# Silu in a convolution and attention block: one table function, or half the sum and its tanh

## Chip, cores, metric

One core of one Trainium2 chip. The metric is the device time of one execution in microseconds; several executions of the same program are run and their median is taken. A profile is of one execution.

Names used below: PE is TensorE, DVE is VectorE, ACT is ScalarE, POOL is GpSimd, SP is SyncE, whose queue issues nearly all DMAs. SBUF is the on-chip working memory, PSUM the eight banks that PE writes its products to. L130 is line 130 of the kernel.

## What is computed

Everything is fp32, on eight images of 512 channels and 32 x 32 positions. Layer 0 is a block of convolutions with attention, added to its input; layer 1 is a masked and permuted 1x1 convolution, also added to its input. Both take a group norm of their input first. Cut to what matters here:

```python
def cbs(x, w, p, pad):                       # convolution, batch norm in eval form, silu
    return silu(bn_eval(conv2d(x, w, pad), p))

def bot_attention(x, qkv_w, rw, rh):         # 4 heads of 64, 1024 positions
    q, k, v = conv2d(x, qkv_w, 0) ...
    logits = einsum('bhdi,bhdj->bhij', q, k + r) * HD ** (-0.5)
    return einsum('bhij,bhdj->bhdi', softmax(logits), v)

t = cbs(x, cv1_w, cv1_bn, 0)                 # 512 -> 512 channels
ys = [t[:, :256], t[:, 256:]]
for i in range(2):
    yi = ys[-1]
    z = cbs(yi, m_cv1_w[i], m_cv1_bn[i], 1)  # 3x3
    z = bot_attention(z, m_qkv_w[i], m_rw[i], m_rh[i])
    z = silu(bn_eval(conv2d(z, m_cv2_w[i], 0), m_cv2_bn[i]))
    ys.append(yi + z)
return cbs(concatenate(ys), cv2_w, cv2_bn, 0)
```

Silu is s * sigmoid(s) with s = scale * x + bias, where scale and bias come from the batch norm of the channel. It stands behind four convolutions: cv1, the 3x3 convolution of each of the two blocks, the 1x1 convolution behind each attention, and cv2.

## The kernel before

The 128 partitions carry channels; the free dimension carries positions, in halves of 512, as a PSUM bank holds 512 fp32 numbers. An image's activations that live longer go through buffers in device memory (`y_dram`, `x2_dram`).

*The slots.* Each image passes two attention blocks; a slot is one block of one image, and images run in pairs, so that there are 16 slots. A slot has four units (`Unit`): one pair of heads and one half of the positions each. A unit runs eight steps `t`. `logits` (L428) makes two PSUM banks of logits on PE (L435), ACT copies them to SBUF (`st`, L441), and DVE keeps a running maximum (`mx`, L446). `top` and `spread` transpose the maximum, reduce it (L455) and spread it into PSUM as `mb` (L462). `soften` (L464) adds `mb` on DVE (L466), takes exp on ACT (L467) and sums on POOL (L470, L472). `values` multiplies with v on PE (L478). `finish` makes the denominators (L490), their reciprocal (L492) and the product into `q` (L493).

*The work between.* A slot's softmax runs for one image while the other work is fed in between its steps, from a list with estimated costs in microseconds (`slot_filler`, `advance`): for the next slot `conv3` (the 3x3 convolution by transformed rows, six products with additions on DVE, L262 to L297) and `project` (q, k and v); for the slot before `conv_m2` (L340); and, from a background list, `conv1` (L201) of later images, `conv2` (L366) and `last` of finished ones. So every kind of Silu falls between copies and exps of a softmax. The order in which each engine executes is fixed when the program is built. The first two images' `start_conv` (L841) runs ahead of any softmax.

*Silu.* `bn_silu` (L129) is one ACT operation, with scale and bias read from the columns of `bn_s` and `bn_b`. Its callers:

- `start_conv` and `conv1`: from a PSUM bank into a tile `t` (named y), which SP stores to `y_dram`; 8 per image, 512 elements each.
- `conv3`: in place on `z` in SBUF, 2 per block, 1024 elements each.
- `conv_m2`: from a bank into `t` (m2s), to which DVE then adds the residual (L354), into `ybuf` or `res`; 4 per block, 512 elements.
- `conv2`: from a bank into `t` (cv2s), to which DVE adds the residual (L380), before the statistics of the second group norm (L139); 8 per image, 512 elements.

That makes 28 per image, 224 in all. ACT evaluates functions from a table set that has to be loaded; where an operation needs another set than the one before, the built program has a load (ACT_TABLE_LOAD in the trace), shown under the line of the operation that it precedes: L130 or L467.

*Buffers.* `half_tile` (L71) gives tiles of 512 elements from the pool `tp`, which has three in turn; besides the callers above `finish` takes one for the reciprocal. The pool `wt` has three tiles of 544 elements for temporaries of `conv3`. Banks come from `ps_f`, five in turn.

*Parameters.* `small_parameters` (L496) makes `bn_s` and `bn_b` once, at the start.

Of the kernel before, what the change touches and what calls it, by code (L numbers as in the profile page):

```python
# [16 lines left out]
AF = mybir.ActivationFunctionType  # L17
ALU = mybir.AluOpType
# [7 lines left out]
IT = 2  # L26
F = 32
HW = F * F
HALF = 512
# [6 lines left out]
BN_CV1, BN_CV2, BN_M1, BN_M2, BN_ALL = 0, 4, 8, 12, 16  # L36
# [3 lines left out]
def conv_preact_kernel(ctx: ExitStack, tc: tile.TileContext, x, cv1, cv2, mcv1, qkv, mcv2, bn, rw, rh, conv, s_in, t_in, out):  # L40
    nc = tc.nc
    stt = nc.vector.scalar_tensor_tensor

    def pool(name, bufs, **kw):
        return ctx.enter_context(tc.tile_pool(name=name, bufs=bufs, **kw))
# [10 lines left out]
    wm = pool("wm", 1)  # L56
    gy = pool("gy", 4)
    gr = pool("gr", 2)
    tp = pool("tp", 3)
    wt = pool("wt", 3)  # L60
    ps_m = pool("ps_m", 1, space=PSUM)
    ps_o = pool("ps_o", 1, space=PSUM)
    ps_f = pool("ps_f", 5, space=PSUM)
# [1 line left out]
    def pair(p, tag, name):  # L65
        return p.tile([P, 2, HALF], F32, tag=tag, name=name)

    def bank(name):
        return ps_f.tile([P, HALF], F32, tag="bank", name=name)

    def half_tile(name):  # L71
        return tp.tile([P, HALF], F32, tag="t", name=name)
# [7 lines left out]
    def weights(name, shape, src):  # L80
        t = wp.tile([P, *shape], F32, tag="w", name=name)
        load(t, src)
        return t
# [42 lines left out]
    bn_s = const.tile([P, BN_ALL], F32, name="bn_s")  # L126
    bn_b = const.tile([P, BN_ALL], F32, name="bn_b")

    def bn_silu(dst, src, col):  # L129
        nc.scalar.activation(dst, src, AF.Silu, bias=bn_b[:, col : col + 1], scale=bn_s[:, col : col + 1])  # L130


    class GroupNorm:
# [42 lines left out]
    class Image:  # L176
# [24 lines left out]
        def conv1(self, h, tiles, order=(1, 0)):  # L201
            n = self.n
            for cp in order:
                w = weights(f"w_cv1_{n}_{h}_{cp}", (CT, 256), cv1[cp])
                for co in range(IT):
                    ps = bank(f"cv1_{n}_{cp}_{co}_{h}")
                    yield from accumulate(ps, [(w[:, k, ts(co, P)], tiles[k // 2][:, k % 2]) for k in range(CT)])
                    t = half_tile(f"y0_{n}_{cp}_{co}_{h}")
                    bn_silu(t, ps, BN_CV1 + IT * cp + co)
                    load(y_dram[n][cp][:, co, ts(h, HALF)], t)  # L210
# [7 lines left out]
        def conv3(self, i):  # L218
            n = self.n
            name = f"{n}_{i}"  # L220
            groups = ybuf.rearrange("p c r x -> p (c r x)").rearrange("p (g r x) -> p g r x", r=4, x=F)
            d = [groups[:, 0:NGR, r] for r in range(4)] + [groups[:, 1 : NGR + 1, r] for r in range(2)]

            def temp(nm):
                return wt.tile([P, NGR, F], F32, tag="wt", name=f"{nm}_{name}")

            def plane():
                plane_count[0] += 1
                return planes[plane_count[0] % 4]

            def inner(u):
                return u[:, :, 1 : F + 1]

            def product(r, u):
                w = weights(f"w_m1_{name}_{r}", (IT, IT, 3, P), w_m1[i][r])
                ps = bank(f"m1_{name}_{r}")
                terms = [(c, dx) for c in range(IT) for dx in range(3)]
                for co in range(IT):
                    for j, (c, dx) in enumerate(terms):
                        nc.tensor.matmul(  # L240
                            ps[:, ts(co, 256)].rearrange("p (t x) -> p t x", x=F),
                            w[:, co, c, dx],
                            u[:, 9 * c : 9 * c + 8, dx : dx + F],
                            start=(j == 0),
                            stop=(j == len(terms) - 1),
                        )
                        if j % 3 == 2 and (co, j) != (1, 5):
                            yield 1.33
                yield 1.33
                self.ps = ps  # L250

            z = self.z = qp.tile([P, IT, HW], F32, tag="z", bufs=1, name=f"z_{name}")
            y4 = z.rearrange("p c (t j x) -> p (c t) j x", j=4, x=F)
            y = [y4[:, :, j] for j in range(4)]

            def tx(ap):
                return ap.rearrange("p (g x) -> p g x", x=F)

            mm, ss, dd = (pair(wm, q, f"{q}_{name}") for q in ("mm", "ss", "dd"))

            a, b = temp("a"), temp("b")
            stt(a, d[2], -4.0, d[4], ALU.mult, ALU.add)  # L262
            stt(b, d[1], -4.0, d[3], ALU.mult, ALU.add)
            u1, u2 = plane(), plane()
            nc.vector.tensor_tensor(inner(u1), a, b, ALU.add)
            nc.vector.tensor_tensor(inner(u2), a, b, ALU.subtract)

            a, b = temp("a2"), temp("b2")
            nc.vector.tensor_tensor(a, d[4], d[2], ALU.subtract)
            nc.vector.tensor_tensor(b, d[3], d[1], ALU.subtract)  # L270
            u3, u4 = plane(), plane()
            stt(inner(u3), b, 2.0, a, ALU.mult, ALU.add)
            stt(inner(u4), b, -2.0, a, ALU.mult, ALU.add)
            yield from product(1, u1)
            nc.scalar.copy(mm[:, 0], self.ps)
            yield from product(2, u2)

            u0, u5 = plane(), plane()
            nc.gpsimd.tensor_tensor(inner(u0), d[0], d[2], ALU.subtract)
            nc.gpsimd.tensor_tensor(inner(u5), d[5], d[3], ALU.subtract)  # L280
            stt(inner(u0), inner(u0), 4.0, a, ALU.mult, ALU.add)
            stt(inner(u5), b, -4.0, inner(u5), ALU.mult, ALU.add)
            nc.vector.tensor_tensor(ss[:, 0], mm[:, 0], self.ps, ALU.add)
            nc.vector.tensor_tensor(dd[:, 0], mm[:, 0], self.ps, ALU.subtract)
            yield from product(3, u3)
            nc.scalar.copy(mm[:, 1], self.ps)
            yield from product(4, u4)
            nc.vector.tensor_tensor(ss[:, 1], mm[:, 1], self.ps, ALU.add)
            nc.vector.tensor_tensor(dd[:, 1], mm[:, 1], self.ps, ALU.subtract)
            stt(y[1], tx(dd[:, 1]), 2.0, tx(dd[:, 0]), ALU.mult, ALU.add)  # L290
            stt(y[2], tx(ss[:, 1]), 4.0, tx(ss[:, 0]), ALU.mult, ALU.add)
            nc.vector.tensor_tensor(ss[:, 0], ss[:, 0], ss[:, 1], ALU.add)
            stt(dd[:, 0], dd[:, 1], 8.0, dd[:, 0], ALU.mult, ALU.add)
            yield from product(0, u0)
            nc.vector.tensor_tensor(y[0], tx(self.ps), tx(ss[:, 0]), ALU.add)
            yield from product(5, u5)
            nc.vector.tensor_tensor(y[3], tx(self.ps), tx(dd[:, 0]), ALU.add)  # L297
            for co in range(IT):
                bn_silu(z[:, co], z[:, co], BN_M1 + IT * i + co)


        def project(self, i):
# [193 lines left out]
    def small_parameters():  # L496

        nc.scalar.dma_start(out=bn_sb, in_=bn)
        nc.scalar.dma_start(out=rw_sb, in_=rw)
        nc.scalar.dma_start(out=rh_sb, in_=rh)  # L500
        nc.scalar.dma_start(out=s_sb[:, 0], in_=s_in)
        nc.scalar.dma_start(out=s_sb[:, 1], in_=t_in)
        nc.vector.tensor_scalar_add(bn_b, bn_sb[:, 3], 1e-3)
        nc.gpsimd.tensor_tensor(bn_s, bn_b, mhalf, ALU.pow)
        nc.vector.tensor_tensor(bn_s, bn_s, bn_sb[:, 0], ALU.mult)
        nc.vector.tensor_tensor(bn_b, bn_sb[:, 2], bn_s, ALU.mult)
        nc.vector.tensor_tensor(bn_b, bn_sb[:, 1], bn_b, ALU.subtract)

    def positions(i):
        for hp in range(IT):  # L510
            t = pair(stp, "st", f"r_{i}_{hp}")
            nc.gpsimd.tensor_tensor(
                flat(t).rearrange("p (r c) -> p r c", c=F),
                rw_sb[:, i, hp].unsqueeze(1).to_broadcast([P, F, F]),
                rh_sb[:, i, hp].unsqueeze(2).to_broadcast([P, F, F]),
                ALU.add,
            )
            load(r_dram[i][:, hp], flat(t))
# [300 lines left out]


    small_parameters()

    def start(im, pool_, tag):
# [164 lines left out]
```

## Times and profile before

| | us |
|---|---|
| three runs | 3569.73, 3575.05, 3577.51; median 3575.05 |
| profiled execution | 3581.82 |
| its span, first to last instruction | 3580.1 |
| PE, DVE, ACT, POOL busy | 3333.1, 2144.3, 1790.1, 1160.5 |
| table loads on ACT | 276 of 1.283 each |
| Silu on ACT, 192 of 512 elements | 49.8 + 49.8 + 49.6 |
| Silu on ACT, 32 of 1024 elements | 38.7 |
| mean granted clock of PE | 0.97 of full speed |

Busy time is the time in which the profiler has an instruction of the engine under way. Matmuls are pipelined, so their busy time holds latency too, and a busy PE is not PE at its peak. A group's row names line, engine, operation, what is written and read, shapes and count; behind the first bar are the busy time in us and the mean of one in ns, behind the second the idle time of the engine just before these instructions and what released it. The chain is followed back from the last instruction: at each step to whatever ended its wait, or else to the instruction before it on its engine. In the timeline and in the chain in order of time, the first number is the start in us, the second the duration.

### The profile page before, as it was taken

Reading aid. Unit: us, or ns where it says so; the run is one execution under the profiler, and the core shown is the slowest. Engines: PE = TensorE matmul, PEld = TensorE weight load, DVE = VectorE, ACT = ScalarE, POOL = GpSimd, SP = SyncE. Lnnn points to the kernel's source line nnn. Section 1 sums busy time; section 2 is a strip of 40 time slices with the busy share of each in tenths; the row PEclk is TensorE's granted clock in tenths of the full one; section 3 lists DMA queues with packets and bytes.
Section 4 is the critical chain, followed back from the end, with each engine's and each line's share of the span. In section 5 each row is a group of like instructions: output and inputs, shape, how many; then the busy total and the mean of one; then the engine's idle time right before and its main releaser. Section 6 shows DMA issues by size and latency. Waiting matters only on the chain.

```text
span 3580.1 us, 32601 instructions
## 1 busy us (share of the span) xinstructions
PE 3333.1 (93%) x11716; PEld 1569.7 (44%) x11716; DVE 2144.3 (60%) x2589; ACT 1790.1 (50%) x2337; POOL 1160.5 (32%) x523
## 2 busy tenths in 40 slices
PE   6999999988999999999999999989999999999988
PEld 3645344343444444344444434344444444354333
DVE  4436565466755565586756566686756566676642
ACT  3045764745555544544555544644555544645631
POOL 2014323233432333333432333333432333333330
PEclk9899999999999999999999999999999999999999
DMA  8552341321323141332323142332222141322355
GB/s 285 205 194 80 117 154 65 108 94 37 104 76 109 65 149 63 105 119 100 110 76 108 65 144 68 122 114 98 103 83 106 65 145 64 130 98 89 115 167 176
DMA packets 142289, 400.29 MB, mean 112 GB/s; under 512 B 13104, under 2 KB 14384, under 8 KB 142128
## 3 DMA queue, kind: packets, MB, share of 16 engines
q1 hardware_dynamic: 141408, 397.99, 32.5%
q8 instruction: 92, 1.51, 0.2%
q14 instruction: 69, 0.57, 0.0%
q10 hardware_dynamic: 720, 0.23, 0.0%
HBM read 318.47 MB, written 79.69 MB: 111 GB/s over the span
## 4 chain that ended last, share of the span: by engine, by line
PE 68%; DVE 13%; issue 7%; ACT 7%; DMA 3%; POOL 2%; SPq 0%; ACTq 0%; POOLq 0%; DVEq 0%
PE cv L171 14%; PE lg L435 11%; PE po L478 10%; PE m L240 9%; PE qk L171 6%; PE l L171 6%; PE v L329 3%; DVE mx L446 3%; DVE st L466 2%; ACT st L441 2%; ACT st L467 2%; PE m L171 2%; PE den L490 2%; PE mt L454 2%; PE mb L462 1%
## 5 line engine op out<-in xcount | busy, mean ns | idle before, releaser
L472 POOL TENSOR_TENSOR sum<-sum,st 128x1024 f32<-128x1024 f32 x384 | 925.3, 2410 | 1009.6 <-ACT st L467 976.1
L467 ACT ACTIVATE st<-st 128x1024 f32<-128x1024 f32 x512 | 538.5, 1056 | 699.3 <-DVE st L466 691.9
L441 ACT COPY st<-lg 128x512 f32<-128x512 f32 x1024 | 536.6, 594 | 477.5 <-PE lg L435 441.3
L446 DVE TENSOR_TENSOR mx<-mx,lg 128x512 f32<-128x512 f32 x768 | 482.1, 680 | 474.7 <-ACT st L441 474.6
L435 PE MATMUL lg<-q,k 64*128 64x512 f32 x2048 | 641.0, 632 | 43.0 <-DVE mx L446 31.3
L466 DVE TENSOR_TENSOR st<-st,mb 128x1024 f32<-128x1024 f32 x512 | 609.8, 1211 | 78.3 <-PE mb L462 78.2
L478 PE MATMUL po<-st,v 128*64 128x512 f32 x2048 | 536.4, 621 | 51.6 <-ACT st L467 42.4
L240 PE MATMUL m<-plane,w_m 128*128 128x256 f32 x2304 | 546.4, 391 | 19.0 <-DVE mx L446 14.2
L240 PEld LDWEIGHTS m<-plane,w_m 128*128 128x128 f32 x2304 | 437.6, 194 | 157.9 <-issue 47.1
L171 PE MATMUL cv<-y,w_cv 128*128 128x512 f32 x1024 | 476.3, 607 | 12.2 <-DVE mx L446 6.9
L470 POOL TENSOR_TENSOR sum<-st,st 128x1024 f32<-128x1024 f32 x64 | 152.3, 2380 | 894.0 <-ACT st L467 887.8
L435 PEld LDWEIGHTS lg<-q,k 64*128 64x128 f32 x2048 | 210.5, 188 | 458.8 <-issue 298.3
L171 PEld LDWEIGHTS cv<-y,w_cv 128*128 128x128 f32 x1024 | 185.7, 191 | 266.1 <-issue 233.9
L478 PEld LDWEIGHTS po<-st,v 128*64 128x64 f32 x2048 | 116.0, 136 | 371.5 <-issue 179.7
L171 PE MATMUL cv<-x,w_cv 128*128 128x512 f32 x512 | 242.7, 623 | 25.9 <-ACT x L165 14.7
L492 DVE RECIPROCAL rb<-den 128x512 f32<-128x512 f32 x64 | 214.7, 3354 | 67.0 <-PE den L490 62.2
L171 PE MATMUL qk<-z,w_qkv 128*128 128x512 f32 x512 | 235.7, 603 | 12.3 <-DVE mx L446 12.3
L171 PE MATMUL l<-x,w_l 128*128 128x512 f32 x512 | 239.3, 614 | 2.4 <-ACT x L165 2.4
L130 ACT ACT_TABLE_LOAD x138 | 177.1, 1283 | 10.5 <-PE cv L171 3.3
L467 ACT ACT_TABLE_LOAD x136 | 174.5, 1283 | 2.4
L455 DVE TENSOR_REDUCE nm<-mt 128x4 f32<-128x512 f32 x128 | 82.5, 684 | 152.8 <-PE mt L454 152.8
L171 PEld LDWEIGHTS cv<-x,w_cv 128*128 128x128 f32 x512 | 97.5, 198 | 155.9 <-issue 112.7
(143 smaller groups left out, 2375.2 us busy)
## 6 DMA issues: line engine op xcount, KB each, us to landing
w_m<-w_m SPq DMA_DIRECT2D x96, 768.0 KB, 4.5
w_cv<-in_cv SPq DMA_DIRECT2D x92, 512.0 KB, 3.5
y<-y SPq DMA_DIRECT2D x64, 512.0 KB, 4.8
x<-in_x SPq DMA_DIRECT2D x56, 512.0 KB, 4.6
y<-y SPq DMA_DIRECT2D x64, 256.0 KB, 3.4
k<-r SPq DMA_DIRECT2D x32, 512.0 KB, 3.5
res<-y SPq DMA_DIRECT2D x32, 512.0 KB, 4.0
xr<-in_x SPq DMA_DIRECT2D x32, 512.0 KB, 4.1
```

Source lines behind the costliest of these rows:

```text
L130: nc.scalar.activation(dst, src, AF.Silu, bias=bn_b[:, col : col + 1], scale=bn_s[:, col : col + 1])
L171: nc.tensor.matmul(ps, w, moving, start=(n == 0), stop=(n == len(terms) - 1))
L240: nc.tensor.matmul(ps[:, ts(co, 256)].rearrange("p (t x) -> p t x", x=F), w[:, co, c, dx], u[:, 9 * c : 9 * c + 8, dx : dx + F], start=(j ...
L435: nc.tensor.matmul(lg[h], self.k[r, ts(t, P)], self.q[r, self.hp, ts(self.half, HALF)], start=True, stop=True)
L441: nc.scalar.copy(st[:, h], lg[h])
L446: in_turn(nc.vector.tensor_tensor(self.mx[:, h], so_far[:, h], lg[h], ALU.max))
L466: in_turn(nc.vector.tensor_tensor(st, st, flat(self.mb), ALU.add))
L467: nc.scalar.activation(st, st, AF.Exp)
L470: nc.gpsimd.tensor_tensor(flat(self.acc), flat(self.st[0]), st, ALU.add)
L472: nc.gpsimd.tensor_tensor(flat(self.acc), flat(self.acc), st, ALU.add)
L478: nc.tensor.matmul(self.po[HD * h : HD * h + HD], self.v[:, t, ts(h, HD)], self.st[t][:, h], start=(t == 0), stop=(t == KT - 1),)
L492: nc.vector.reciprocal(rb, den)
```

## The change

Silu is computed in another way. With h = s / 2, silu(s) = s * sigmoid(s) = h + h * tanh(h). The scale and bias columns are halved once. Then ACT makes tanh(h) into a tile `th` and h into the destination, and DVE makes (th + 1) * h in place. Tanh and exp are found in one table set. In `conv3`, where the destination is 1024 wide, the calls are cut into halves of 512, because `th` is a half tile. `tp` goes from three tiles to four, `wt` from three to two.

```diff
@@ pools
-    tp = pool("tp", 3)
-    wt = pool("wt", 3)
+    tp = pool("tp", 4)
+    wt = pool("wt", 2)
@@ bn_silu
     def bn_silu(dst, src, col):
-        nc.scalar.activation(dst, src, AF.Silu, bias=bn_b[:, col : col + 1], scale=bn_s[:, col : col + 1])
+
+        th = half_tile("th")
+        kw = dict(bias=bn_b[:, col : col + 1], scale=bn_s[:, col : col + 1])
+        nc.scalar.activation(th, src, AF.Tanh, **kw)
+        nc.scalar.activation(dst, src, AF.Identity, **kw)
+        stt(dst, th, 1.0, dst, ALU.add, ALU.mult)
@@ conv3
-            for co in range(IT):
-                bn_silu(z[:, co], z[:, co], BN_M1 + IT * i + co)
+            for h in range(2):
+                for co in range(IT):
+                    part = z[:, co, ts(h, HALF)]
+                    bn_silu(part, part, BN_M1 + IT * i + co)
@@ small_parameters
+        nc.vector.tensor_scalar(bn_s, bn_s, 0.5, None, ALU.mult)
+        nc.vector.tensor_scalar(bn_b, bn_b, 0.5, None, ALU.mult)
```

`stt` is `nc.vector.scalar_tensor_tensor`: here (th + 1.0) * dst, on DVE, with both tensors in SBUF.

## The prediction

> **What bounds the kernel now.** I read the page first: the engines' shares, then the chain that ended last.
>
> ```profile
> PE 3333.1 (93%) x11716; PEld 1569.7 (44%) x11716; DVE 2144.3 (60%) x2589; ACT 1790.1 (50%) x2337; POOL 1160.5 (32%) x523
> ...
> PE 68%; DVE 13%; issue 7%; ACT 7%; DMA 3%; POOL 2%; SPq 0%; ACTq 0%; POOLq 0%; DVEq 0%
> ```
>
> TensorE (PE) carries 68% of the chain. What another engine does costs only the part of it that the chain passes through. From these two lines: VectorE (DVE) is busy 60% and holds 13% of the chain, so 13/60 = 0.22 of its work is paid for; for ScalarE (ACT) it is 7/50 = 0.14. These two shares price everything below.
>
> Next the waits of TensorE alone.
>
> ```profile
> PE po L478 <- ACT st L467: 42.4, 35, 3.3
> PE lg L435 <- DVE mx L446: 31.3, 25, 4.1
> ```
>
> Columns: total us, times, longest. Over the whole view, waits that ended on DVE sum to about 154 us and on ACT to about 78 us. And behind the exp (L467) that ACT lets TensorE wait for, ACT itself waited 692 us for the DVE addition L466. DVE is the dearer engine to load.
>
> Then the groups that the change touches, and their kin (busy us, mean ns of one, idle before and its releaser).
>
> ```profile
> L130 ACT ACT_TABLE_LOAD x138 | 177.1, 1283 | 10.5 <-PE cv L171 3.3 <-PE m L171 3.2 <-issue 1.8
> L467 ACT ACT_TABLE_LOAD x136 | 174.5, 1283 | 2.4
> L130 ACT ACTIVATE m2s<-m,bn_b,bn_s 128x512 f32<-128x512 f32 x64 | 49.8, 778 | 77.7 <-PE m L171 76.8
> L130 ACT ACTIVATE z<-z,bn_b,bn_s 128x1024 f32<-128x1024 f32 x32 | 38.7, 1238 | 35.2 <-DVE z L297 35.1
> ...
> L380 DVE TENSOR_TENSOR xr<-xr,cv2s 128x512 f32<-128x512 f32 x64 | 58.1, 908 | 106.6 <-ACT cv2s L130 106.5
> L354 DVE TENSOR_TENSOR ybuf<-res,m2s 128x512 f32<-128x512 f32 x32 | 36.2, 1140 | 52.8 <-ACT m2s L130 34.1 <-DMA res<-y 18.7
> L354 DVE TENSOR_TENSOR res<-res,m2s 128x512 f32<-128x512 f32 x32 | 27.9, 876 | 56.1 <-DMA res<-y 34.3 <-ACT m2s L130 21.7
> L293 DVE SCALAR_TENSOR_TENSOR dd<-dd 128x512 f32<-128x512 f32 x16 | 10.8, 678 | 0.0
> ```
>
> The loads are 352 us of ACT, a fifth of its work. L380 and L354 are 512 elements from two SBUF operands like the new multiply, yet dearer than L293's 678 ns. The timeline says why: such an operation that starts under a GpSimd (POOL) operation lasts until that one ends, and costs 0.71 us when it doesn't.
>
> ```profile
> 1320.05 2.75 POOL L472 TENSOR_TENSOR sum<-sum,st 128x1024 f32<-128x1024 f32 x1 [5.97 <-ACT st L467]
> 1320.51 2.87 DVE L266 TENSOR_TENSOR plane<-a,b 128x544 f32<-128x544 f32 x1
> ...
> 1760.27 0.71 DVE L266 TENSOR_TENSOR plane<-a,b 128x544 f32<-128x544 f32 x1
> ```
>
> Last, where loads lie on the chain. Read in order of time, the chain holds 45 pieces of load, 52.7 us, and 39 of Silu, 27.4 us (29 of them m2s). They gather at a slot's change, where conv_m2 feeds the next conv3:
>
> ```profile
> 1504.66 0.78 ACT m2s L130
> ...
> 1505.45 1.28 ACT L467
> ...
> 1508.77 1.28 ACT L130
> ...
> 1510.07 0.79 ACT m2s L130
> ...
> 1510.88 2.39 DVE ybuf L354
> ```
>
> **The change, part by part.** *ACT.* The built order of the changed kernel has 1 table load where that of before has 276, as the trace has (138 + 136 + 2): 275 x 1.283 = 353 us go. The 224 Silus go: 49.8 + 49.8 + 49.6 + 38.7 = 188 us. 256 calls (z in four pieces instead of two) bring 512 ACT operations of 512 elements at the Silu's 0.777 us, the same form with the same pointers: 398 us. Net -143 us, times 0.14 = **-20 us**. Bounds: the loads' own 52.7 us on the chain against 39 second operations x 0.78 = 30 us gives -22; nothing gained if the chain moves aside, 0.
>
> The skill's page ScalarE: Activation LUTs, section What ACT_TABLE_LOAD costs, adds about 1380 ns of drain to each load's 1283. Here the load at 1505.45 follows an operation that ended 0.02 us earlier and the exp starts 0.01 us after it: no drain shows. With the drain, 380 us more would go, x 0.14 = -53 us, and the sum below would turn into a gain of 23 us; I go by the row.
>
> *DVE.* 256 scalar_tensor_tensor are added. Ends: 0.678 us (L293, same operation and size, never under POOL) and 0.955 us (L380 and L354 together: 122.2 us / 128). The 128 behind m2s and cv2s stand just ahead of such an addition, which would have paid the wait for POOL itself: 0.678 each, 87 us. The 64 for y and 64 for z pay in full: 0.955 each, 122 us. Sum 209 us (174 to 244), times 0.22 = **+45 us** (38 to 53).
>
> The skill's page SBUF — State Buffer, section Who interferes with whom, speaks against the change: a DVE operation with two SBUF inputs fully blocks against a GpSimd one that reads SBUF. As an estimate from it, all 256 would meet POOL in 32% of cases and wait half of 2.41 us, 1.07 us each, 274 us, +59 us instead of +45; the rows agree in kind, and I keep the rows' figure.
>
> *New waits on DVE.* y had nothing on DVE; now its multiply stands in DVE's queue and waits for ACT, with mx (L446) and the additions st (L466) behind it, for which PE's lg and ACT's exp wait. Nearest rows: L380 waited for ACT 106.5 us over 64, L354 55.8 us over 64. At 0.87 us, 64 of them idle DVE 56 us (1.66 us would make 106). Against that, m2s and cv2s already let DVE wait; with a load before them it was 1.28 + 0.78 = 2.06 us, now 1.56 until the multiply may start: 138 x 128/224 x 0.5 = 39 us less. Net +17 us x 0.22 = **+4** (0 to +15). For z the four multiplies end 8 x 0.777 + 0.68 = 6.9 us after L297; at 1393 us the softmax addition behind them started 6.6 us after it, so +0.3 us x 16 = 5 us, x 0.22 = **+1**.
>
> *Costed at nothing.* A PSUM bank is held for two reads, 1.56 us, against 2.06 or 0.78 before; five banks cover it, and if not, ACT's share has it. The buffers: each call now takes two of four where it took one of three, so a Tanh may have to wait for the store of y two calls back; the stores land 3.4 us after issue and four products take 8 x 0.43 = 3.4 us per call, with attention between: covered; uncovered, 64 x about 1 us of ACT x 0.14 = +9. SP's queue gets no new transfer, but its 64 y stores, which already waited 170 us for ACT y, wait one multiply longer with weight loads behind them; TensorE waits on DMA hardly at all (5.4 us for y), so nothing. wt with two buffers: its readers and writers are on DVE, in order. Two 16-column DVE operations at the start: 0.3 us.
>
> **Sum**: -20 + 45 + 4 + 1 = +30 us. The profiled execution took 3581.8 us (span 3580.1 and 1.7 around it), so 3612; the median shown is 6.8 us under it, and I forecast on the median: 3575 + 30 = **3605 us**.
>
> **The rivals.**
> *ACT's relief wins (faster).* Place: the slot's change above and the 22 loads ahead of exps on the chain. Price: -52.7 + 30 = -22 us, the multiplies hidden in DVE's 40% idle time: 3553. For: 162 us of DVE's idle time stand right before L380 and L354, where half the multiplies go. Against: with the multiply, a silu with a load on this path costs 1.56 + 0.68 = 2.24 us for 2.06. It decides when DVE's share falls below 22/209 = 0.11, half of what the chain shows.
> *Even.* Both shares shrink alike, as TensorE's 93% covers the rest: 3575.
> *POOL collisions (slower by more).* If the multiplies meet POOL's sums as often as L265 does (22.2 us / 16 = 1.39 us), 356 us x 0.22 = 78, -20 + 78 + 5 = +63: 3638. For: exp releases POOL and the multiplies stand among the exps. Against: L380's 45 of 64 at 0.67 us.
> *The loads stay* (Tanh outside exp's set): ACT +210 us x 0.14 + 45 = +74, 3649. The built order speaks against it; under 1 in 100.
>
> **How the numbers follow.** Forecast (about 3585 to 3625) 0.45; ACT's relief 0.28; even 0.12; collisions, with the loads staying, 0.15. Under 0.2% (7 us) can't be told from no change here. Faster 0.28, same 0.12, slower 0.60. The range reaches a little past the relief, to 3545 (its -22 and 8 us for chain that reroutes my way), and past the collisions, to 3650; the forecast's own range is 3585 to 3625.
>
> **What would show it.** Right: one load; ACT busy near 1647 us, DVE near 2353; DVE's share of the chain up by a point or more; the multiplies' mean between 0.68 and 0.96 us. The ACT step is wrong if TensorE's waits on exp shrink by much more than 20 us; the DVE step if its waits on mx don't grow. The forecast falls if the slot's change from the first m2s to conv3's first plane gets over 1 us shorter with DVE's other waits as before.

## The result, and the profile after

The changed kernel takes 3621.04 us (median of 4, 3613.73 to 3625.92) against 3576.28 us before: a ratio of 1.0124, 95% interval 1.0100 to 1.0149. That is 45 us slower, where 30 had been forecast. The profiled execution took 3625.92 us. First the shares of the engines and the chain, on the page of the changed kernel:

```profile
PE 3313.6 (91%) x11716; PEld 1576.7 (44%) x11716; DVE 2449.0 (68%) x2847; ACT 1606.4 (44%) x2350; POOL 1182.7 (33%) x523
...
PE 52%; DVE 26%; issue 8%; ACT 6%; DMA 5%; POOL 2%; SPq 0%; ACTq 0%; POOLq 0%; DVEq 0%
```

ACT lost 184 us of work, DVE gained 305, and DVE's share of the chain doubled from 13% to 26%. Next the groups that answer to those shown of before (busy us, mean ns of one, idle before and its releaser):

```profile
L135 DVE SCALAR_TENSOR_TENSOR m2s<-th,m2s 128x512 f32<-128x512 f32 x64 | 90.8, 1423 | 20.8 <-ACT m2s L134 20.7
L387 DVE TENSOR_TENSOR xr<-xr,cv2s 128x512 f32<-128x512 f32 x64 | 89.4, 1397 | 1.7
...
L135 DVE SCALAR_TENSOR_TENSOR cv2s<-th,cv2s 128x512 f32<-128x512 f32 x64 | 67.3, 1052 | 87.9 <-ACT cv2s L134 87.9
L135 DVE SCALAR_TENSOR_TENSOR z<-th,z 128x512 f32<-128x512 f32 x64 | 56.4, 895 | 23.2 <-ACT z L134 23.1
L135 DVE SCALAR_TENSOR_TENSOR y<-th,y 128x512 f32<-128x512 f32 x64 | 56.1, 876 | 67.0 <-ACT y L134 67.0
L361 DVE TENSOR_TENSOR res<-res,m2s 128x512 f32<-128x512 f32 x32 | 51.7, 1622 | 3.1 <-DMA res<-y 2.7
L361 DVE TENSOR_TENSOR ybuf<-res,m2s 128x512 f32<-128x512 f32 x32 | 46.8, 1462 | 5.9 <-DMA res<-y 5.4
```

The 256 multiplies (L135) take 270.6 us, 1.06 us each. And the additions of the residual, which the change does not touch, grew: L380, now L387, from 58.1 to 89.4 us, and L354, now L361, from 64.1 to 98.5. The timeline of the changed kernel shows one slot's change (start us, duration us; x2 is two operations in a row in one line):

```profile
1523.43 0.77 ACT L134 ACTIVATE m2s<-m,bn_b,bn_s 128x512 f32<-128x512 f32 x1
1524.09 1.05 ACT L474 ACTIVATE st<-st 128x1024 f32<-128x1024 f32 x1
1524.23 0.69 DVE L135 SCALAR_TENSOR_TENSOR m2s<-th,m2s 128x512 f32<-128x512 f32 x1 [0.33 <-ACT m2s L134]
...
1525.29 5.12 POOL L479 TENSOR_TENSOR sum<-sum,st 128x1024 f32<-128x1024 f32 x2 [9.05 <-ACT st L474]
1525.70 0.78 ACT L134 ACTIVATE m2s<-m,bn_b,bn_s 128x512 f32<-128x512 f32 x1
1525.80 2.40 DVE L361 TENSOR_TENSOR ybuf<-res,m2s 128x512 f32<-128x512 f32 x1 [0.87 <-DMA res<-y]
...
1528.12 2.84 DVE L135 SCALAR_TENSOR_TENSOR m2s<-th,m2s 128x512 f32<-128x512 f32 x1
...
1531.00 0.69 DVE L361 TENSOR_TENSOR ybuf<-res,m2s 128x512 f32<-128x512 f32 x1
```

The same place in the kernel before, behind the Silu at 1504.66 and the load at 1505.45 that the prediction shows:

```profile
1506.75 2.00 ACT L467 ACTIVATE st<-st 128x1024 f32<-128x1024 f32 x2
1507.12 0.68 DVE L354 TENSOR_TENSOR ybuf<-res,m2s 128x512 f32<-128x512 f32 x1
...
1507.94 2.35 POOL L470 TENSOR_TENSOR sum<-st,st 128x1024 f32<-128x1024 f32 x1 [21.93 <-ACT st L467]
```

There the addition was done before POOL began. In the changed kernel, with no load between them, the exp starts as soon as h is made, and 1.2 us later POOL sums. The addition at 1525.80 lasts 2.40 us instead of 0.69 because POOL is at work; then POOL's next sum starts, and the multiply at 1528.12 waits for that one too: 2.84 us. DVE spends 5.2 us on what takes 1.4. Who pays is in the waits of TensorE (total us, times, longest):

```profile
PE po L485 <- ACT st L474: 57.4, 42, 2.9
PE m L245 <- DVE mx L453: 44.5, 22, 4.4
PE m L176 <- DVE mx L453: 34.2, 15, 3.3
```

Over the view, waits that end on mx rise from 89 us to 132; waits for the exp from 42 to 57, and the exp in turn waits longer for DVE's addition (692 us before, 886 now).

**A measure used below.** For each DVE instruction I take what it lasted over the shortest one of its line and tiles, and sum this where it is over 0.15 us. I take it for the time that DVE stood in an operation for POOL: 164 us before, 314 in the changed kernel, and 7 to 11 in the versions below in which POOL sums nothing. A second measure is when POOL's next sum starts after the ACT operation that ends a silu. Before, none of the 64 for m2s and none of the 64 for cv2s started within 2.2 us; the median for m2s was 2.51. In the changed kernel 68% and 43% do, with a median of 1.61 us for m2s.

### The profile page after: what moved, and what is told of

Its sections match the earlier page's. It is cut to its first block, busy times and chain, and to the rows that moved or that the text cites. A ratio compares the mean times of both kernels' runs of the same rounds, so it can differ in the third digit from the quotient of the medians.

```text
span 3624.2 us, 32893 instructions
## 1 busy us (share of the span) xinstructions
PE 3313.6 (91%) x11716; PEld 1576.7 (44%) x11716; DVE 2449.0 (68%) x2847; ACT 1606.4 (44%) x2350; POOL 1182.7 (33%) x523
## 4 chain that ended last, share of the span: by engine, by line
PE 52%; DVE 26%; issue 8%; ACT 6%; DMA 5%; POOL 2%; SPq 0%; ACTq 0%; POOLq 0%; DVEq 0%
PE cv L176 9%; PE m L245 9%; PE po L485 7%; PE lg L442 7%; PE l L176 6%; PE qk L176 6%; DVE st L473 5%; DVE mx L453 5%; DMA x<-in_x 3%; PE v L336 2%; DVE rb L499 2%; ACT st L448 2%; ACT st L474 2%; DVE m2s L135 2%; PE den L497 2%
## 5 line engine op out<-in xcount | busy, mean ns | idle before, releaser
L479 POOL TENSOR_TENSOR sum<-sum,st 128x1024 f32<-128x1024 f32 x384 | 948.0, 2469 | 1072.5 <-ACT st L474 1042.7
L442 PE MATMUL lg<-q,k 64*128 64x512 f32 x2048 | 607.5, 631 | 30.9 <-DVE mx L453 20.2
L245 PE MATMUL m<-plane,w_m 128*128 128x256 f32 x2304 | 555.5, 397 | 52.7 <-DVE mx L453 44.5
L485 PE MATMUL po<-st,v 128*64 128x512 f32 x2048 | 527.6, 620 | 66.1 <-ACT st L474 57.4
L245 PEld LDWEIGHTS m<-plane,w_m 128*128 128x128 f32 x2304 | 445.9, 198 | 188.5 <-DVE mx L453 63.3
L176 PE MATMUL cv<-y,w_cv 128*128 128x512 f32 x1024 | 469.0, 602 | 7.4 <-DMA y<-y 4.5
L442 PEld LDWEIGHTS lg<-q,k 64*128 64x128 f32 x2048 | 203.1, 189 | 426.0 <-issue 300.9
L133 ACT ACTIVATE th<-cv,bn_b,bn_s 128x512 f32<-128x512 f32 x128 | 98.9, 773 | 166.3 <-PE cv L176 166.2
L176 PE MATMUL m<-q,w_m 128*128 128x512 f32 x256 | 133.7, 666 | 34.2 <-DVE mx L453 34.2
L176 PEld LDWEIGHTS l<-x,w_l 128*128 128x128 f32 x512 | 96.9, 197 | 139.0 <-issue 116.5
```

Of the source, the lines that this page charges most:

```text
L133: nc.scalar.activation(th, src, AF.Tanh, **kw)
L176: nc.tensor.matmul(ps, w, moving, start=(n == 0), stop=(n == len(terms) - 1))
L245: nc.tensor.matmul(ps[:, ts(co, 256)].rearrange("p (t x) -> p t x", x=F), w[:, co, c, dx], u[:, 9 * c : 9 * c + 8, dx : dx + F], start=(j ...
L442: nc.tensor.matmul(lg[h], self.k[r, ts(t, P)], self.q[r, self.hp, ts(self.half, HALF)], start=True, stop=True)
L479: nc.gpsimd.tensor_tensor(flat(self.acc), flat(self.acc), st, ALU.add)
L485: nc.tensor.matmul(self.po[HD * h : HD * h + HD], self.v[:, t, ts(h, HD)], self.st[t][:, h], start=(t == 0), stop=(t == KT - 1),)
```

## The experiments

The kernel before was timed anew beside each group: 3577.63 us for the first four, 3579.51 and 3579.54 for the two groups after; the changed kernel's row is that of the result. The other ratios are to these times, with their 95% intervals.

| kernel | us | ratio, interval | DVE waiting in operations, us |
|---|---|---|---|
| before | 3576 to 3580 | | 164 |
| the changed kernel | 3621.0 | 1.0124 (1.0100 to 1.0149) | 314 |
| no multiply | 3536.2 | 0.9886 (0.9873 to 0.9899) | 206 |
| Silu and multiply | 3586.7 | 1.0027 (1.0015 to 1.0039) | 200 |
| half in PSUM | 3577.4 | 1.0002 (0.9991 to 1.0014) | 246 |
| pools alone | 3564.9 | 0.9965 (0.9952 to 0.9977) | 176 |
| all in PSUM | 3556.1 | 0.9934 (0.9921 to 0.9946) | 155 |
| Silu in PSUM | 3552.6 | 0.9911 (0.9891 to 0.9931) | 139 |
| changed, no sums | 3382.3 | 0.9443 (0.9430 to 0.9455) | 11 |
| before, no sums | 3450.2 | 0.9638 (0.9623 to 0.9652) | 7 |
| changed, POOL writes only | 3380.1 | 0.9445 (0.9428 to 0.9462) | 8 |
| Silu in PSUM, pools | 3551.6 | 0.9924 (0.9906 to 0.9942) | 157 |
| all in PSUM, pools of before | 3548.8 | 0.9919 (0.9896 to 0.9941) | 138 |
| loads put back | 3609.5 | 1.0081 (1.0064 to 1.0098) | 227 |

### The two parts apart

No multiply, from the changed kernel:

```diff
         nc.scalar.activation(dst, src, AF.Identity, **kw)
-        stt(dst, th, 1.0, dst, ALU.add, ALU.mult)
```

> The changed kernel with the DVE multiply left out (the destination keeps h, so silu itself is not computed); no table loads, two ACT operations per call. Theory (ACT's part is a relief, DVE's multiply is the whole loss): about 20 us under the kernel before, 3540 to 3570, DVE busy near 2150 us, ACT near 1610. Rival (two ACT operations in a row hold up the path as much as the loads did, so ACT's part brings nothing): 3576 or more.

3536.2 us, 41 under the kernel before: ACT's part is a relief, of up to twice the size that I gave it. This version has the changed pools too, and they alone make the kernel before 13 us faster (below), so how much of the 41 is ACT's is open. DVE was busy 2190 us, ACT 1605. The multiply costs 3621 - 3536 = 85 us. Its absence does not undo all collisions: the additions at L354, now L360, take 87 us where they took 64 before.

Silu and multiply, from the kernel before:

```diff
         nc.scalar.activation(dst, src, AF.Silu, bias=bn_b[:, col : col + 1], scale=bn_s[:, col : col + 1])
+        stt(dst, dst, 1.0, dst, ALU.mult, ALU.max)
...
-            for co in range(IT):
-                bn_silu(z[:, co], z[:, co], BN_M1 + IT * i + co)
+            for h in range(2):
+                for co in range(IT):
+                    part = z[:, co, ts(h, HALF)]
+                    bn_silu(part, part, BN_M1 + IT * i + co)
```

> The kernel before, table loads and Silu kept, z cut in halves of 512, and after each Silu one DVE scalar_tensor_tensor of 512 elements with two SBUF operands that changes nothing (max(1.0 * y, y)). Theory (the DVE multiply is the loss, a new wait for ACT included): 45 to 70 us over the kernel before, 3620 to 3645, the added operation near 1.06 us each as in the changed kernel. Rival (DVE's 40% idle time hides it, and the loss comes from the order or from ACT): under 3595.

3586.7 us, only 9 more: the theory as I had it, that the multiply alone is the loss, falls. With the loads kept, as many multiplies with two SBUF operands (here the same tile twice) are nearly hidden, though DVE is 191 us busier. The groups of this kernel say what differs:

```profile
L131 DVE SCALAR_TENSOR_TENSOR m2s<-m2s 128x512 f32<-128x512 f32 x64 | 66.5, 1043 | 47.0 <-ACT m2s L130 47.0
...
L383 DVE TENSOR_TENSOR xr<-xr,cv2s 128x512 f32<-128x512 f32 x64 | 44.0, 687 | 1.1
```

Here the multiply of m2s takes 1.04 us on average instead of 1.42, and L383 never meets POOL: 0.69 us instead of 1.40. It took 0.91 in the kernel before; here the multiply ahead of it takes the wait (0.93 us for cv2s). As before, no sum of POOL starts within 2.2 us of the end of a Silu of m2s or cv2s. The multiplies do not keep clear of POOL altogether, with a mean of 0.90 us over all 256. The new theory: a table load between a silu and the exp behind it held the exp back, and with it POOL's sum, just long enough for DVE to finish. The change took this shield away and put more work where it had stood.

### Collisions taken away, the number of operations kept

Half in PSUM, from the changed kernel:

```diff
-        nc.scalar.activation(dst, src, AF.Identity, **kw)
-        stt(dst, th, 1.0, dst, ALU.add, ALU.mult)
+        h = dst if src is dst else src
+        nc.scalar.activation(h, src, AF.Identity, **kw)
+        stt(dst, th, 1.0, h, ALU.add, ALU.mult)
```

> The changed kernel with h written back in place to its PSUM bank for y, m2s and cv2s (192 of 256 calls), so that the multiply has one SBUF operand and one in PSUM; the same number of operations. Theory (collisions with POOL are a part of the loss): these multiplies take 0.68 to 0.70 us each, DVE busy falls by about 85 us from 2449, and at 0.22 to 0.26 of it the time falls to about 3600. Rival (the number of DVE operations and their place count, collisions cost nothing): 3621, within 8 us. Rival (banks held longer stall TensorE): over 3630.

3577.4 us: 44 us less than the changed kernel with as many operations, more than the 20 expected, though DVE's busy time fell by 64 us and not by 85. The groups of this kernel:

```profile
L388 DVE TENSOR_TENSOR xr<-xr,cv2s 128x512 f32<-128x512 f32 x64 | 81.3, 1270 | 1.7
L362 DVE TENSOR_TENSOR res<-res,m2s 128x512 f32<-128x512 f32 x32 | 60.0, 1881 | 8.7 <-DMA res<-y 8.3
...
L136 DVE SCALAR_TENSOR_TENSOR m2s<-th,m 128x512 f32<-128x512 f32 x64 | 43.3, 678 | 24.8 <-ACT m L135 24.8
```

The multiply with one operand in PSUM costs 0.68 us and meets POOL no more; the additions behind it, with two SBUF operands, still do, and L362 for longer than before (1.88 us for 1.62).

All in PSUM carries this on for m2s and cv2s; the 64 multiplies of z keep two SBUF operands:

```diff
-                    t = half_tile(f"m2s_{name}_{co}_{h}")
-                    bn_silu(t, ps, BN_M2 + IT * i + co)
+                    bn_silu(ps, ps, BN_M2 + IT * i + co)
                     dst = y_rows(co, h) if i == 0 else res[:, co]
-                    nc.vector.tensor_tensor(dst, res[:, co], t, ALU.add)
+                    nc.vector.tensor_tensor(dst, res[:, co], ps, ALU.add)
...
-                    t = half_tile(f"cv2s_{n}_{h}_{co}")
-                    bn_silu(t, ps, BN_CV2 + co)
-                    nc.vector.tensor_tensor(res[:, c], res[:, c], t, ALU.add)
+                    bn_silu(ps, ps, BN_CV2 + co)
+                    nc.vector.tensor_tensor(res[:, c], res[:, c], ps, ALU.add)
```

> As k3_half_in_psum, and for m2s and cv2s the multiply also writes to the PSUM bank and the addition of the residual (L361, L387) reads it there, so that no operation of these two chains has two SBUF operands. Theory (DVE waits for POOL in each operation with two SBUF operands): the 101 us that these additions still took over their shortest in k3 go, DVE busy falls to about 2285 us, the time at 0.22 by about 20 to 3555. Rival (the bank, now held until DVE has added, makes TensorE wait): 3580 or more.

3556.1 us, as expected. Its additions:

```profile
L386 DVE TENSOR_TENSOR xr<-xr,cv 128x512 f32<-128x512 f32 x64 | 43.6, 681 | 1.5
...
L361 DVE TENSOR_TENSOR ybuf<-res,m 128x512 f32<-128x512 f32 x32 | 21.9, 683 | 8.0 <-DMA res<-y 7.5
```

The idea without the tanh, Silu in PSUM, is the last diff on the kernel before, with its Silu.

> The kernel before with its Silu and table loads, where the Silu of m2s and cv2s is written in place to the PSUM bank and the residual is added from there. Theory (before, the table load between Silu and exp kept POOL's sums away from these additions, so there is little to gain): the 37 us that they took over their shortest go, at 0.22 about 8 us: 3562 to 3575. Rival (collisions cost the kernel before as much as the changed one): under 3550. Rival (banks): over 3585.

3552.6 us, 27 less than before where I expected 8. The direction fits; the size is between my theory and its rival, and why 25 us less of DVE's waiting bring 27 us here stays open.

### POOL's sums, and what of them it is

Changed, no sums, and before, no sums, with the same diff:

```diff
-                nc.gpsimd.tensor_tensor(flat(self.acc), flat(self.st[0]), st, ALU.add)
-            elif t > 1:
-                nc.gpsimd.tensor_tensor(flat(self.acc), flat(self.acc), st, ALU.add)
+                nc.gpsimd.memset(flat(self.acc), 1.0)
```

> The changed kernel with POOL's sums left out: each unit's denominator is a constant tile of ones, so the attention output is not normalised rightly. To be compared with k8_before_no_sums. Theory (collisions with POOL are the whole loss): without them the changed kernel is as fast as k8 or faster, k7 minus k8 between -35 and +5 us; the multiplies take 0.68 us each. Rival (the loss lies in the number of DVE operations or in their waits for ACT): k7 is 30 us or more over k8.

> The kernel before with POOL's sums left out in the same way: denominators are constant. Theory: a little faster than before, 3545 to 3575, as its collisions are few and POOL is off the chain for 98% of it; DVE busy about 2144 - 130 = 2015 us. Rival (POOL itself bounds the softmax): under 3500.

Without the sums the order turns round: the changed kernel takes 3382 us, the one before 3450. What the change brings is 68 us, more than the 35 that I had as its bound, and with POOL's sums it is a loss of 45. I had put the kernel before without sums at 3545 or more and missed: the sums cost it 129 us as well. POOL was near 2% of the chain, and the page did not show this price, as a part of it stands inside DVE's operations. Another part may be TensorE's clock: with the sums it was granted 0.966 to 0.974 of full speed, without them 0.983 to 0.986, and the lg matmul took 622 to 623 ns for 631 to 632. As an estimate, 1.4% to 1.8% of TensorE's 3300 us is some 50 to 60 us at most; why the clock differs stays open. The two versions without sums have the same clock, so the 68 us between them does not come from it. These two also take POOL's work away, and what waits for it, so a third one keeps POOL busy and takes away its reads only:

```diff
-                nc.gpsimd.tensor_tensor(flat(self.acc), flat(self.st[0]), st, ALU.add)
+                nc.gpsimd.tensor_copy(self.acc[:, 0, :1], st[:, :1])
+                for _ in range(2):
+                    nc.gpsimd.memset(flat(self.acc), 1.0)
             elif t > 1:
-                nc.gpsimd.tensor_tensor(flat(self.acc), flat(self.acc), st, ALU.add)
+                nc.gpsimd.tensor_copy(self.acc[:, 0, :1], st[:, :1])
+                for _ in range(2):
+                    nc.gpsimd.memset(flat(self.acc), 1.0)
```

> The changed kernel, where each of POOL's sums is replaced by a one-column copy that waits for the exp as the sum did, and two writes of ones over the whole tile, so that POOL is busy at the same places for about 2.1 us but reads almost nothing; denominators are constant. Theory (DVE's operations with two SBUF operands wait for POOL's reads): the multiplies fall to about 0.7 us and the time to 3380 to 3420, near k7_after_no_sums. Rival (POOL's activity or the release of the st tiles by it costs the time, not its reads): 3550 or more.

3380.1 us, as expected, at a clock of 0.985 to 0.987. Groups of this kernel, POOL first:

```profile
L483 POOL MEMSET sum<- 128x1024 f32 x768 | 730.7, 951 | 44.6
...
L481 POOL COPY sum<-st 128x1 f32<-128x1 f32 x384 | 98.4, 256 | 921.9 <-ACT st L474 911.3
```

```profile
L135 DVE SCALAR_TENSOR_TENSOR m2s<-th,m2s 128x512 f32<-128x512 f32 x64 | 44.1, 688 | 22.0 <-ACT m2s L134 21.6
```

POOL is busy 1046 us, against 1183 in the changed kernel, and starts behind the exps just the same, but it writes and hardly reads; the multiply with two SBUF operands takes 0.69 us. So it is POOL's reads that DVE's second SBUF operand waits for. The Trainium skill states this on its page SBUF — State Buffer, section Who interferes with whom; these runs agree.

### The shield itself

Loads put back, from the changed kernel, at m2s and cv2s:

```diff
...
         nc.scalar.activation(dst, src, AF.Identity, **kw)
+        if load_back:
+            one_col = small.tile([P, 1], F32, tag="back", name="back")
+            nc.scalar.activation(one_col, th[:, :1], AF.Silu)
...
```

> The changed kernel with table loads put back behind m2s and cv2s: after h, ACT makes Silu of one column of th into a tile that nobody reads, which makes the build place a load before it and another before the next exp (189 loads more, 242 us of ACT). Theory (a load between silu and exp kept POOL's next sum 2.5 us away, and its removal let POOL run into DVE's multiply and addition): the additions of the residual take 0.8 to 0.95 us instead of 1.40 and 1.54, the multiplies of m2s about 1.0 instead of 1.42, and the time is no more than 3625 in spite of the loads. Rival (the loads' removal has nothing to do with the collisions): the durations stay, and the time rises by 242 x 0.14 = 34 us or more, to 3655 and over.

3609.5 us: ACT works 265 us more (1606 to 1872), for loads that serve nothing, and the kernel is about 12 us faster. Its rows:

```profile
L390 DVE TENSOR_TENSOR xr<-xr,cv2s 128x512 f32<-128x512 f32 x64 | 67.9, 1060 | 1.4
L138 DVE SCALAR_TENSOR_TENSOR m2s<-th,m2s 128x512 f32<-128x512 f32 x64 | 62.8, 982 | 26.0 <-ACT m2s L134 25.7
...
L364 DVE TENSOR_TENSOR res<-res,m2s 128x512 f32<-128x512 f32 x32 | 34.5, 1084 | 8.5 <-DMA res<-y 8.2
```

The durations fall to 1.06 us for L390, 0.98 for the multiply, and 1.00 for L364 over its two groups (1.08 and 0.91); the additions not as far as I had put them (0.80 to 0.95). POOL's next sum starts within 2.2 us after 5% of m2s (68% without the loads) and 23% of cv2s (43%). So loads that hold the exp back do keep POOL's sums off these operations. It is not the shield of before as it was: a call has two loads and a small Silu here, and the median until POOL's next sum is 4.02 us for m2s, against 2.51 before. How much of the 45 us the lost shield accounts for is not shown.

### The pools

Pools alone: the kernel before with `tp` at 4 and `wt` at 2. Two more runs cross the pools with the PSUM versions.

> The kernel before with only the pools changed (tp 4 tiles, wt 2). Theory: no difference, 3576 within 8 us. Rival (two wt tiles hold up conv3's additions, or the built order shifts): over 3590.

> k6_silu_in_psum with the changed kernel's pools (tp 4, wt 2). Theory (the two gains of k4 and k6, 12 and 27 us, come from different causes and add): about 3540. Rival (each is a shift of the built order, and they don't add): 3550 to 3580.

> k5_all_in_psum with the pools of before (tp 3, wt 3). Theory (the pools' gain of k4 holds with tanh too): about 3568. Rival (tp is relieved there, wt with three tiles is as good): 3556 within 8 us, or under.

The pools make the kernel before 13 us faster (3564.9), which neither theory had; with Silu in PSUM they bring nothing (3551.6 against 3552.6, where I expected 3540), and with all in PSUM the pools of before are, if anything, better (3548.8 against 3556.1, ranges overlapping, where I expected 3568). Each of these builds also has another order of instructions. What of the 13 us is the buffers and what the order was not taken apart; I read differences of some 10 us between builds as no proof of a mechanism; that holds for the 12 us of the loads put back and the 9 us of Silu and multiply too, whose weight lies in DVE's durations. The four versions whose additions read PSUM too, 3549 to 3556 us, beat both kernels; the simplest is Silu in PSUM, which touches two places.

## Why the prediction came out as it did

The direction was right, and 3621 us lies near the upper end of the forecast's own range, 3585 to 3625. The sum was -20 + 45 + 4 + 1; the runs give -41 for the changed kernel without its multiply and +85 for the multiply. That the sum came within 15 us is in part luck: the two misses, 21 us and 35 us (85 for 50), point opposite ways. Of the signs named, one load, more waiting for mx and a larger share of DVE came; the multiplies' mean, 1.06 us, lies over its bound of 0.96, and ACT and DVE were busy 1606 and 2449 us, not 1647 and 2353.

*ACT, -20.* Too small: up to -41. Its work fell by 184 us rather than 143, as its operations overlap by 44 us more than before: Tanh and Identity in a row (starts mostly 0.66 to 0.68 us apart at 0.77 us each), and others between which a load stood. Whether the flat share of the chain, 0.14, was too low is not shown: 41/184 = 0.22, but 28/184 = 0.15 if the pools' 13 us are taken off, and DVE's waiting rose by 42 us in the same run. No drain beside the loads' 1283 ns shows in any run: a load starts 17 to 18 ns after the operation before it at the median, and the next one 11 to 13 ns after the load.

*DVE, +45.* The step that failed is "The 128 behind m2s and cv2s stand just ahead of such an addition, which would have paid the wait for POOL itself". They took 1.42 and 1.05 us, and the additions behind them grew as well, by 66 us in all. In the kernel that keeps its loads the step holds for cv2s, where the addition fell from 0.91 to 0.69 us; without the loads it fails: POOL's sums can come back to back, and two DVE operations in a row then wait for one each (2.40 and 2.84 us in the timeline above). Of the multiplies priced at 0.955, those for y and z were near it (0.88 and 0.90). Over all 256 the mean was 1.06 us where I had 0.82; the estimate from the skill's page SBUF — State Buffer, section Who interferes with whom, gave 1.07 and would have been the better price, though it had one mean for multiplies that took from 0.88 to 1.42 and did not foresee the additions' growth. One reading was loose: in the lines shown at 1320 us DVE's operation does not last until POOL's ends but 0.58 us beyond it, so it waits and then does nearly all of its own work.

*The share, 0.22.* One price for all of DVE's time hid two. The multiplies by themselves are close to free: +9 us for 256 in the kernel that keeps its loads, where DVE's waiting rose by 36 us only, and without the sums the changed kernel gains although DVE does 165 us more. Time in which DVE stands for POOL cost at least that share of it, but no one price holds. Where operands moved and the number of operations stayed, it is 44 us for 68 of it from the changed kernel to half in PSUM, 21 for 90 from there to all in PSUM, and 27 for 25 from the kernel before to Silu in PSUM. Without the sums it is 239 for 303 and 129 for 157, but the higher clock is in these.

*What I had not in the sum at all.* The rows of before were taken as the rate of collisions, as if removing the loads left it alone. The loads themselves helped to keep it low. A reading that was to be had in advance: in the timeline of before, the exp behind m2s starts 1.3 us late, and POOL's sum only behind it.

*New waits on DVE, +4 and +1.* The idle time before y, cv2s, m2s and z multiplies is 67, 88, 21 and 23 us; before the change L380 and L354 waited 162 us for ACT. That is 37 us more where I had 17 for the first three and 5 for z. The version without sums has the same waits (66, 88, 22 and 30) and is 68 us faster than its counterpart, so they are not the loss.

*The rivals.* "POOL collisions" named the mechanism, with a chance of 0.15, and asked for a mean of 1.39 us; it came to 1.06 for the multiplies, and the additions made up much of the rest. "ACT's relief wins" has its relief, larger than priced, but the multiplies are not hidden in DVE's idle time while POOL sums. The table loads went as the built order said: one is left.

*Costed at nothing.* Two reads of a bank cost next to nothing: TensorE's waits that end on ACT's y and m2s sum to 5.2 us in the changed kernel. The pools were not neutral in the kernel before, as the runs above show.

## To carry to other kernels

An operation that only costs time may hold back an engine that would get in another's way; before taking it out, look in the timeline for what starts behind it and which operations get done before that. The mean of a group with a wide spread is two prices: split it by whether another engine was at work, and price the added operations by where they will stand. If DVE's two-operand work runs beside POOL's sums, give it one operand in PSUM; here that was worth 27 us on the kernel before and 65 us on the changed one.

## What the runs showed of the hardware that was not expected

A GpSimd that writes a whole tile for 1.9 us (two writes of 951 ns) behind an exp doesn't slow a VectorE operation with two SBUF operands (0.69 us), while one that reads two tiles makes it last up to 2.85 us. Adding 242 us of table loads to ScalarE, with 26 us of small operations, didn't make the changed kernel slower but some 12 us faster, and took 87 us off what VectorE waits in its operations. With POOL's sums gone, or replaced by writes, TensorE was granted 0.983 to 0.987 of its clock, against 0.966 to 0.974 in the two kernels.
